# Half-product attention scores for all pairs of inner blocks, summed up in two PSUM banks

## The chip, the core and the metric

The kernel runs on one core of a Trainium2 chip. The metric is the device time of one execution in microseconds; lower is better. The median of three runs of the kernel before is 2275.2 us (2273.95 to 2275.97).

## What is computed

A stack of graph layers works on 3327 nodes with 256 features in float32, with one dense adjacency matrix. Layer 2, which the change touches, is masked dot-product attention followed by a residual and a layer norm:

```python
q = x @ Wq.T + bq
k = x @ Wk.T + bk
v = x @ Wv.T + bv
scores = q @ k.T / sqrt(256)
scores = where(adj > 0, scores, -9e15)
att = softmax(scores, axis=-1) @ v
x = layernorm(x + elu(att))
```

The other layers are a cosine attention (layer 0), a graph attention (layer 1) and three graph attentions in a row (layers 3a, 3b, 3c). They are the same in both kernels.

## The kernel before

The nodes are padded to 3328 and lie in 26 tiles of 128 (NT = 26) and in seven blocks of 512 (NB = 7, the last one 256 wide). A layer walks over its blocks `b` of query nodes, and within a block over the 26 tiles `j` of key nodes. One step (b, j) is one 128x512 tile of attention weights: key nodes on the partitions, query nodes along the columns. Since the weights come out transposed, they can be the left operand of the product with the values.

For layer 2 the query side is folded: `block2` makes `g` (gT in the profile), the 256 x 512 matrix that the keys' features `FT` are multiplied with. A score tile is thus a sum of two products of 128x128 weights with 512 columns, one for each half of the 256 features. `weights2` (lines 682 to 697) does that in one PSUM bank, lets ScalarE take the exponential out of the bank (L694), and VectorE multiplies by the mask (`masked`, L496).

Two neighbouring tiles j = 2p and 2p + 1 form a pair p. Seen as a pair, the scores are a 2x2 block product: two key tiles by two feature halves, times two feature halves by two query halves of 256 columns. Strassen's scheme in Winograd's form needs seven products of 128x128 by 256 columns for it, where the direct way needs eight (four of 512 columns). `pair_weights` (from L636) does it with seven. It needs sums of the query quarters, t1 to t4 (`sum_queries`, once per block, L583 to L586), and of the key quarters, s1 to s4 (`sum_keys`, L627 to L630, 128x128 each).

`by_pairs` (L607) says which pairs are made so. In the kernel before these are nine of the 13 pairs in the inner blocks 1 to 5 and four in block 0; the rest go through `weights2`. The nine are those for which a place was found to keep the key sums through the whole layer (`KPAIRS`: tags of weights that are no longer used, two "u" buffers, and unused columns of FT). `KSTEPS` says at which step of the layer each of them is summed.

`pair_weights` of before computes the products two to a bank, each into columns of its own: four banks, 7 products. ScalarE copies the first product out (L665). VectorE then adds the others one at a time to the running sums in SBUF (L666, L667, L668, L671, L672, L673, L676: seven adds of 256 columns, each with one operand in PSUM). Each of the two tiles then gets one exponential over 512 columns (L660) and one mask. It is a generator with three parts: the first four products when the step before the pair is made, the next two at the pair's first step, the last one at the second.

The attention product with the values is itself done in the seven-product way: `sums` (L883 to L886) makes four combinations of a pair's two weight tiles, and `products` (L935) issues 14 products of 128x128 by 128 or 129 columns for a pair, accumulated over the block in four PSUM banks of the pool `ps_o` (5 banks). The right operands come in part from DRAM (`fetch_tsum`, L857). All score work uses the pool `ps_b`: three banks, used in turn.

At step s the loop makes weights up to step s + 2 (`make_to`, LA = 2) before it issues the products of step s; they are issued at odd j for two tiles. A block that is done is normalised by `finish`, a generator that is advanced once per step of the next block: on ScalarE four scalings (L1181) and four exponentials for the ELU (L1247), on VectorE the joining of the seven products (L967 to L979), the ELU's adds (L1253, L1262), the statistics (L1109, L1110), the layer norm (L1291), and sums for the following layer.

Apart from the first few steps, a scheduler in the compiler orders each engine's instructions, so that instructions of several such parts lie between each other. The order on an engine is fixed when the program is built. Where two engines use the same PSUM bank the framework orders them by semaphores.

Of the kernel before, what the change touches and what calls it, by code (L numbers as in the profile page):

```python
# [8 lines left out]
F32 = mybir.dt.float32  # L9
# [4 lines left out]
AF = mybir.ActivationFunctionType  # L14
ALU = mybir.AluOpType
# [4 lines left out]
P = 128  # L20
D = 256
# [12 lines left out]
def gnn_stack(ctx: ExitStack, tc: tile.TileContext, a: dict, N: int, out: bass.AP):  # L34
# [8 lines left out]
    nc = tc.nc  # L43
    NT = (N + P - 1) // P
    NP = NT * P
    NB = (NP + CH - 1) // CH
# [11 lines left out]
    wts = ctx.enter_context(tc.tile_pool(name="wts", bufs=1))  # L58
    cols = ctx.enter_context(tc.tile_pool(name="cols", bufs=2))
    mpool = ctx.enter_context(tc.tile_pool(name="mpool", bufs=2))  # L60
    work = ctx.enter_context(tc.tile_pool(name="work", bufs=2))
# [4 lines left out]
    def bank(name):  # L66
        return ps_b.tile([P, CH], F32, tag="pb", name=name)
# [3 lines left out]
    start = tc.manual_schedule(  # L71
        engines={engines.PE, engines.Activation, engines.DVE, engines.Pool}
    )
# [419 lines left out]
    def masked(b, j, t_):  # L493
        wd = bw(b)
        e = work.tile([P, CH], F32, tag="e", name="e", bufs=9)
        nc.vector.scalar_tensor_tensor(  # L496
            e[:, :wd], t_[:, :wd], 0.0, mask(b, j), ALU.add, ALU.mult
        )
        return e
# [78 lines left out]
    def sum_queries(b):  # L578
# [13 lines left out]
    gsum, ksum = {}, {}  # L592
    KPAIRS = {
        1: "w_l0_wqk",
        2: "row_1",
        4: "scratch1",
        5: "scratch2",
        7: "u",
        8: "u",
        10: None,  # L600
        11: "w_l1_w",
# [3 lines left out]
    KSTEPS = {4: 5, 6: 7, 8: 8, 11: 10, 14: 1, 16: 2, 18: 4, NT + 14: 11, NT + 16: 12}  # L605

    def by_pairs(L, b, p):  # L607
        return L.key == "2" and b < NB - 1 and p in (KPAIRS if b > 0 else (5, 7, 8, 10))

    def keys_of(p):  # L610

# [4 lines left out]

    def sum_keys(p):
        a11, a12, a21, a22 = keys_of(p)
        if KPAIRS[p] is None:
            s1, s2, s3, s4 = wsum  # L620
        else:
            if KPAIRS[p] == "u":
                x = work.tile([P, 4, P], F32, tag="u", name="ksum", bufs=2)
            else:
                x = wts.tile([P, 4, P], F32, tag=KPAIRS[p], name="ksum")
            s1, s2, s3, s4 = (x[:, i, :] for i in range(4))
        nc.vector.tensor_tensor(s3, a11, a21, ALU.subtract)  # L627
        nc.vector.tensor_tensor(s1, a21, a22, ALU.add)
        nc.vector.tensor_tensor(s2, s1, a11, ALU.subtract)
        nc.vector.tensor_tensor(s4, a12, s2, ALU.subtract)  # L630
        ksum[p] = s1, s2, s3, s4

    def pair_weights(b, p):

        g, off = gq[b]
        b11, b12, b21, b22 = (g[:, h, i * D : (i + 1) * D] for h in range(2) for i in range(2))  # L636
        t1, t2, t3, t4 = gsum[b]
        a11, a12, a21, a22 = keys_of(p)
        s1, s2, s3, s4 = ksum[p]
        add = ALU.add  # L640
        x = [work.tile([P, CH], F32, tag="a", name="ex2", bufs=4) for _ in range(2)]
        c12, c22 = (t[:, D:] for t in x)

        def two(*pairs):
            ps = bank("ps2")
            for i, (l, r) in enumerate(pairs):
                nc.tensor.matmul(ps[:, i * D : (i + 1) * D], l, r, start=True, stop=True)
            return ps

        def add_two(out, x, ps):  # L650

            nc.vector.tensor_tensor(
                out.rearrange("p (i q) -> p i q", i=2),
                x.unsqueeze(1).to_broadcast([P, 2, D]),
                ps.rearrange("p (i q) -> p i q", i=2),
                add,
            )

        def weights(k):
            nc.scalar.activation(x[k], x[k], AF.Exp, bias=off, scale=1.0 / D**0.5)  # L660
            return masked(b, 2 * p + k, x[k])

        m12 = two((a11, b11), (a12, b21))
        m67 = two((s2, t2), (s3, t3))
        nc.scalar.copy(c22, m12[:, :D])  # L665
        nc.vector.tensor_tensor(x[0][:, :D], c22, m12[:, D:], add)  # L666
        nc.vector.tensor_tensor(c12, c22, m67[:, :D], add)  # L667
        nc.vector.tensor_tensor(c22, c12, m67[:, D:], add)  # L668
        yield
        m45 = two((a22, t4), (s1, t1))  # L670
        nc.vector.tensor_tensor(c12, c12, m45[:, D:], add)  # L671
        nc.vector.tensor_tensor(x[1][:, :D], c22, m45[:, :D], add)  # L672
        nc.vector.tensor_tensor(c22, c22, m45[:, D:], add)  # L673
        yield weights(1)
        m3 = two((s4, b22))
        nc.vector.tensor_tensor(c12, c12, m3[:, :D], add)  # L676
        yield weights(0)

    def weights2(b, j):

# [196 lines left out]
    def sums(b, e1, e2):  # L877

        hw = bw(b) // 2
        s3, s1, s2, s4 = (x[:, i, :hw] for x in two_slots("ssum") for i in range(2))  # L880
        e11, e21 = e1[:, :hw], e1[:, hw : 2 * hw]
        e12, e22 = e2[:, :hw], e2[:, hw : 2 * hw]
        nc.vector.tensor_tensor(s3, e11, e21, ALU.subtract)  # L883
        nc.vector.tensor_tensor(s1, e21, e22, ALU.add)
        nc.vector.tensor_tensor(s2, s1, e11, ALU.subtract)  # L885
        nc.vector.tensor_tensor(s4, e12, s2, ALU.subtract)  # L886
        return e11, e12, e22, s1, s2, s3, s4
# [19 lines left out]
    def products(pos, b, p, es, v):  # L907
        e11, e12, e22, s1, s2, s3, s4 = es
        t = tsums.pop((b, p))
        b1, b2 = v[2 * p], v[2 * p + 1]  # L910
        where = places(pos, b)


        todo = []
        x = {1: e11, 2: e12, 3: s4, 4: e22, 5: s1, 6: s2, 7: s3}
        y = {
            1: b1[:, H:],
            2: b2[:, H:],
            3: b2[:, :H],
            4: t[:, 3 * H + 1 :],  # L920
            5: t[:, : H + 1],
            6: t[:, H + 1 : 2 * H + 1],
            7: t[:, 2 * H + 1 : 3 * H + 1],
        }

        for k, i in (
            (1, 0), (1, 1), (2, 0), (7, 0), (7, 1), (6, 0), (6, 1),
            (2, 1), (5, 0), (5, 1), (4, 0), (4, 1), (3, 0), (3, 1),
        ):
            if i < len(where[k]):  # L930
                g, o = where[k][i]
                todo.append((g, o, x[k][:, i * P : (i + 1) * P], y[k]))
        banks = [t[0] for t in todo]
        for i, (g, o, x, y) in enumerate(todo):
            nc.tensor.matmul(  # L935
                o,
                x,
                y,
                start=(p == 0 and g not in banks[:i]),
                stop=(p == NT // 2 - 1 and g not in banks[i + 1 :]),  # L940
            )
# [539 lines left out]
    steps = [(L, b, j) for L in layers for b in range(NB) for j in range(NT)]  # L1481
    made = deque()

    pairs = {}

    def make(s):
        if s >= len(steps):
            return
        L, b, j = steps[s]
        make_weights(L, b, j)  # L1490
        if j % 2 and by_pairs(L, b, (j + 1) // 2):
            pairs[b, j + 1] = pair_weights(b, (j + 1) // 2)
            next(pairs[b, j + 1])

    cells = {}

# [3 lines left out]
    def make_weights(L, b, j):  # L1500
        if strassen(L, b) and j % 2 == 0 and kept.get((L.key, j // 2)) != b:
            fetch_tsum(L.key, b, j // 2)
        if by_pairs(L, b, j // 2):
            made.append(next(pairs[b, j - j % 2]))
            if j % 2:
                e1, e2 = made.pop(), made.pop()
                made.append(None)
                made.append(sums(b, e1, e2))
        else:
            if L.is_gat:  # L1510
                made.append(L.gat.weights(b, j))
                if deep(L) and strassen(L, b) and in_quad(b, j):
                    made[-1] = cells.setdefault((L.i, b, j // 2), []) if j % 2 else None
                    if j % 4 == 3:
                        v = quad(L.gat.quads, b, j).rearrange("p (a k) c -> p a k c", k=2)
                        for a_, x in enumerate(quad_sums(v)):
                            cells.pop((L.i, b, j // 2 - 1 + a_)).extend(x)
                    return
            else:
                made.append((weights0 if L.key == "0" else weights2)(b, j))  # L1520
            if strassen(L, b) and j % 2:
                e2, e1 = made.pop(), made.pop()
                made.append(None)
                made.append(sums(b, e1, e2))
# [36 lines left out]
    for s, (L, b, j) in enumerate(steps):  # L1561
# [5 lines left out]
        first = L.key == "0" and b == 0  # L1567
# [49 lines left out]
        if end:  # L1617

            k, h = divmod(2 * j, NT)
            for i in (h, h + 1):  # L1620
                for o in range(2 if k else 1):
# [5 lines left out]
                        start=(i == 0),  # L1627
# [70 lines left out]
        if L.key == "1" and (b, j) == (0, 22):  # L1698
            sum_weights(w[L.w])
        if L.key == "2" and b * NT + j in KSTEPS:  # L1700
            sum_keys(KSTEPS[b * NT + j])
        if L.key == "2" and (b, j) == (0, 3):
            sum_queries(0)
        if j == (25 if L.key == "1" else 22) and not end:
# [87 lines left out]
```

## Time and profile before

| | value |
|---|---|
| median of three runs | 2275.2 us |
| profiled execution: own time / span | 2274.9 us / 2273.1 us |
| PE busy | 2246.8 us, 99% |
| VectorE (DVE) busy | 1985.7 us, 87% |
| ScalarE (ACT) busy | 1236.6 us, 54% |
| granted TensorE clock | 0.998 |
| layer 2, about | 801 to 1368 us of the span |
| one inner block of layer 2 | 86 us |

PE is TensorE's matmuls, PEld its weight loads, DVE VectorE, ACT ScalarE, POOL GpSimd, SP the engine that issues DMAs. A group's row reads: line, engine, operation, tiles written <- read, shapes, count, busy time and mean duration, idle time of the engine just before and what ended it. A float32 product is two matmul instructions in the profile, each with its own weight load. Matmuls overlap each other's ends, so their cost in a stream is the distance from start to start and not the duration.

### The profile page before, as it was taken

How to read it: one execution, taken by the hardware profiler on the slowest of the kernel's cores; microseconds unless marked ns; L12 is line 12 of the kernel's file. 1: busy time of each engine (PE TensorE's matmuls, PEld its weight loads, DVE VectorE, ACT ScalarE, POOL GpSimd, SP SyncE). 2: the span in 40 equal slices, each digit the busy share in tenths (PEclk: the TensorE clock that was granted, in tenths of full speed). 3: DMA queues.
4: the chain of work that ended last, by engine and by line, in shares of the span. 5: the costliest groups of instructions: out<-in, count | busy, mean ns of one | idle time of the engine just before them, and what ended most of it. 6: DMA issues, size and time to landing. Idle time of an engine off the chain costs nothing. (4 is left out here: it accounts for less than half of the span.)

```text
span 2273.1 us, 41590 instructions
## 1 busy us (share of the span) xinstructions
PE 2246.8 (99%) x15183; PEld 1999.1 (88%) x15183; DVE 1985.7 (87%) x5407; ACT 1236.6 (54%) x2012; POOL 43.1 (2%) x196
## 2 busy tenths in 40 slices
PE   9999999999999999999999999999999999999997
PEld 7788888888888878888888899999999999999997
DVE  6889999966677767998988989999899999899997
ACT  4677777765455522232322335666666765666663
POOL 0000001000000000000000000000000000000000
PEclk9999999999999999999999999999999999999999
DMA  8655655522322232122122244445435545355542
GB/s 280 198 177 169 200 191 183 177 85 77 91 73 55 70 93 78 57 95 87 57 94 73 75 138 154 142 133 150 133 103 166 142 130 148 106 158 170 152 120 56
DMA packets 186208, 286.13 MB, mean 126 GB/s; under 512 B 80413, under 2 KB 105492, under 8 KB 181396
## 3 DMA queue, kind: packets, MB, share of 16 engines
q1 hardware_dynamic: 185732, 283.22, 41.3%
q8 instruction: 120, 1.97, 0.4%
q14 instruction: 84, 0.69, 0.1%
q10 hardware_dynamic: 272, 0.26, 0.0%
HBM read 228.21 MB, written 38.44 MB: 117 GB/s over the span
## 5 line engine op out<-in xcount | busy, mean ns | idle before, releaser
L787 ACT ACTIVATE re<-u,nrh,th 128x512 f32<-128x512 f32 (+1 forms) x728 | 532.7, 777 | 297.7 <-DVE e L800 146.8
L1657 PE MATMUL po<-v,e 128*128 128x257 f32 x1872 | 422.6, 381 | 1.0 <-ACT p L1181 0.8
L1657 PEld LDWEIGHTS po<-v,e 128*128 128x128 f32 x1872 | 352.6, 190 | 60.9 <-issue 9.8
L935 PE MATMUL po<-tsums,qsum 128*128 128x128 f32 (+1 forms) x2520 | 351.6, 275 | 3.1 <-DVE zs L970 1.2
L800 DVE SCALAR_TENSOR_TENSOR ft<-re,rh,mask 128x512 f32<-128x512 f32 x468 | 337.0, 741 | 3.0 <-ACT re L787 3.0
L935 PEld LDWEIGHTS po<-tsums,qsum 128*128 128x128 f32 x2520 | 315.4, 192 | 4.7 <-DVE qsum L873 1.5
L935 PE MATMUL po<-tsums,ssum 128*128 128x128 f32 (+1 forms) x2082 | 292.7, 276 | 2.7 <-DMA tsums<-t3a_d 1.0
L935 PE MATMUL po<-v,ft 128*128 128x129 f32 x1872 | 286.1, 276 | 0.8 <-DVE ft L800 0.3
L935 PEld LDWEIGHTS po<-tsums,ssum 128*128 128x128 f32 x2082 | 262.2, 192 | 5.7 <-DVE ssum L885 1.8
L935 PEld LDWEIGHTS po<-v,ft 128*128 128x128 f32 x1872 | 251.7, 192 | 5.7 <-DVE ft L800 1.1
L935 PEld LDWEIGHTS po<-v,e 128*128 128x128 f32 x1196 | 172.3, 191 | 37.6 <-issue 23.9
L935 PE MATMUL po<-v,e 128*128 128x129 f32 x1196 | 185.1, 275 | 0.0
L524 ACT ACTIVATE ex<-ps,rq 128x512 f32<-128x512 f32 (+1 forms) x183 | 118.9, 652 | 114.7 <-PE ps L511 111.8
L800 DVE SCALAR_TENSOR_TENSOR e<-re,rh,mask 128x512 f32<-128x512 f32 (+1 forms) x234 | 148.2, 655 | 35.1 <-PE po L1657 24.1
L511 PE MATMUL ps<-ft 128*128 128x512 f32 (+1 forms) x364 | 166.9, 564 | 0.0
L496 DVE SCALAR_TENSOR_TENSOR e<-ex,mask 128x512 f32<-128x512 f32 (+1 forms) x182 | 115.4, 648 | 49.0 <-ACT ex L694 31.8
L525 DVE SCALAR_TENSOR_TENSOR e<-ex,mask 128x512 f32<-128x512 f32 (+1 forms) x183 | 116.5, 642 | 31.0 <-ACT ex L524 30.4
L935 PE MATMUL po<-tsums,ft 128*128 128x128 f32 x936 | 143.5, 275 | 0.1
L686 PE MATMUL ps<-gT,ft 128*128 128x512 f32 (+1 forms) x336 | 129.8, 527 | 0.0
L935 PE MATMUL po<-v,qsum 128*128 128x128 f32 x840 | 128.3, 275 | 0.0
L935 PEld LDWEIGHTS po<-tsums,ft 128*128 128x128 f32 x936 | 123.5, 192 | 0.5 <-ACT p L1181 0.3
L660 ACT ACTIVATE ex<-ex,off 128x512 f32<-128x512 f32 x98 | 67.0, 716 | 101.7 <-DVE ex L676 69.1
(347 smaller groups left out, 3566.7 us busy)
## 6 DMA issues: line engine op xcount, KB each, us to landing
mask<-mask_d SPq DMA_DIRECT2D x30, 1664.0 KB
stage<-in_adj_a SPq DMA_DIRECT2D x78, 512.0 KB
tsums<-t_d SPq DMA_DIRECT2D x152, 256.5 KB
tsums<-t3a_d SPq DMA_DIRECT2D x77, 256.5 KB
tsums<-t3b_d SPq DMA_DIRECT2D x77, 256.5 KB
tsums<-t3c_d SPq DMA_DIRECT2D x77, 256.5 KB
mask_d<-mask SPq DMA_DIRECT2D x6, 1664.0 KB
u<-s_d SPq DMA_DIRECT2D x24, 256.0 KB
```

Source lines behind the costliest of these rows:

```text
L496: nc.vector.scalar_tensor_tensor(e[:, :wd], t_[:, :wd], 0.0, mask(b, j), ALU.add, ALU.mult)
L511: nc.tensor.matmul(ps[:, :wd], FT[j // 4][:, 0, (j % 4) * P : (j % 4 + 1) * P], FT[b][:, 1, :wd], start=True, stop=True,)
L524: nc.scalar.activation(t_[:, c], ps[:, c], AF.Exp, scale=rq[:, j : j + 1])
L525: nc.vector.scalar_tensor_tensor(e[:, c], t_[:, c], 0.0, mask(b, j)[:, c], ALU.add, ALU.mult)
L660: nc.scalar.activation(x[k], x[k], AF.Exp, bias=off, scale=1.0 / D**0.5)
L686: nc.tensor.matmul(ps[:, :wd], FT[j // 4][:, h, (j % 4) * P : (j % 4 + 1) * P], g[:, h, :wd], start=(h == 0), stop=(h == 1),)
L787: nc.scalar.activation(t_[:, :wd], self.u[b][:, :wd], AF.Relu, bias=self.nrh[:, j : j + 1], scale=self.th[:, j : j + 1],)
L800: nc.vector.scalar_tensor_tensor(e[:, :wd], t_[:, :wd], self.rh[:, j : j + 1], mask(b, j), ALU.add, ALU.mult,)
L935: nc.tensor.matmul(o, x, y, start=(p == 0 and g not in banks[:i]), stop=(p == NT // 2 - 1 and g not in banks[i + 1 :]),)
L1657: nc.tensor.matmul(pos[k], e[:, k * P : (k + 1) * P], V[L.i % 2][i], start=(i == 0), stop=(i == NT - 1),)
```

## The change

All pairs of the inner blocks 1 to 5 and the pairs 4 to 12 of block 0 are made from seven half-products. Key sums that aren't kept are computed for each use into a buffer of the tag "e". In `pair_weights` five of the seven products are accumulated one after the other in one half of one bank (`r`): each running sum is copied out by ScalarE before the next product is added to it. The second product takes the other half of that bank. The last two (s1·t1 and s4·b22) are summed up in a second bank (`q`). VectorE adds three times instead of seven. One exponential half is read straight out of the bank.

The parts are issued at other places too: the first at the odd step before the pair (ahead of the end of the pair before), the second and third in the middle of `products` of an earlier pair (before its fifth and tenth product), the last when the pair's second tile is made.

```diff
     def by_pairs(L, b, p):
-        return L.key == "2" and b < NB - 1 and p in (KPAIRS if b > 0 else (5, 7, 8, 10))
+        return L.key == "2" and b < NB - 1 and p < NT // 2 and (b > 0 or p > 3)
...
     def sum_keys(p):
         a11, a12, a21, a22 = keys_of(p)
-        if KPAIRS[p] is None:
+        kept_in = KPAIRS.get(p, "e") if p not in ksum else "e"
+        if kept_in is None:
             s1, s2, s3, s4 = wsum
...
+            elif kept_in == "e":
+                x = work.tile([P, 4, P], F32, tag="e", name="ksum", bufs=9)
...
-        ksum[p] = s1, s2, s3, s4
+        return s1, s2, s3, s4
+
+    inner = deque()
...
-        s1, s2, s3, s4 = ksum[p]
...
+        s1, s2, s3, s4 = ksum[p] if p in ksum else sum_keys(p)
...
-        m12 = two((a11, b11), (a12, b21))
-        m67 = two((s2, t2), (s3, t3))
-        nc.scalar.copy(c22, m12[:, :D])
-        nc.vector.tensor_tensor(x[0][:, :D], c22, m12[:, D:], add)
-        nc.vector.tensor_tensor(c12, c22, m67[:, :D], add)
-        nc.vector.tensor_tensor(c22, c12, m67[:, D:], add)
-        yield
-        m45 = two((a22, t4), (s1, t1))
-        nc.vector.tensor_tensor(c12, c12, m45[:, D:], add)
-        nc.vector.tensor_tensor(x[1][:, :D], c22, m45[:, :D], add)
-        nc.vector.tensor_tensor(c22, c22, m45[:, D:], add)
-        yield weights(1)
-        m3 = two((s4, b22))
-        nc.vector.tensor_tensor(c12, c12, m3[:, :D], add)
-        yield weights(0)
+        def put(out, l, r, first=False):
+            nc.tensor.matmul(out, l, r, start=first, stop=True, skip_group_check=True)
+
+        ps = bank("ps2")
+        r, m2 = ps[:, :D], ps[:, D:]
+        put(r, a11, b11, first=True)
+        put(m2, a12, b21)
+        nc.scalar.copy(c11, r)
+        nc.vector.tensor_tensor(c11, c11, m2, ALU.add)
+        yield
+        put(r, s2, t2)
+        nc.scalar.copy(c12, r)
+        yield
+        put(r, s3, t3)
+        q = bank("ps3")[:, :D]
+        put(q, s1, t1, first=True)
+        nc.scalar.copy(c22, r)
+        nc.vector.tensor_tensor(c22, c22, q, ALU.add)
+        yield
+        put(r, a22, t4)
+        put(q, s4, b22)
+        nc.scalar.activation(c21, r, AF.Exp, bias=off, scale=scale)
+        nc.scalar.activation(c22, c22, AF.Exp, bias=off, scale=scale)
+        e2 = masked(b, 2 * p + 1, x[1])
+        nc.vector.tensor_tensor(c12, c12, q, ALU.add)
+        nc.scalar.activation(x[0], x[0], AF.Exp, bias=off, scale=scale)
+        yield masked(b, 2 * p, x[0]), e2
...
         for i, (g, o, x, y) in enumerate(todo):
+            if i in (4, 9) and inner:
+                next(inner[0])
             nc.tensor.matmul(
...
+        if j % 2 and s + 1 < len(steps):
+            ln, bn, jn = steps[s + 1]
+            if by_pairs(ln, bn, jn // 2):
+                pairs[bn, jn] = pair_weights(bn, jn // 2)
+                next(pairs[bn, jn])
+                inner.append(pairs[bn, jn])
         make_weights(L, b, j)
-        if j % 2 and by_pairs(L, b, (j + 1) // 2):
-            pairs[b, j + 1] = pair_weights(b, (j + 1) // 2)
-            next(pairs[b, j + 1])
```

In the text below, c11, c12, c21 and c22 are the four quarters of a pair's two score tiles; "the c12 copy" is ScalarE's copy into that quarter, ADD11, ADD22 and ADD12 are VectorE's three adds into c11, c22 and c12, and s2·t2 is the product of s2 and t2.

More of the change, by code (lines that the diff above doesn't have):

```diff
@@ L618, in sum_keys @@
         a11, a12, a21, a22 = keys_of(p)
-        if KPAIRS[p] is None:
+        kept_in = KPAIRS.get(p, "e") if p not in ksum else "e"
+        if kept_in is None:
             s1, s2, s3, s4 = wsum
         else:
-            if KPAIRS[p] == "u":
+            if kept_in == "u":
                 x = work.tile([P, 4, P], F32, tag="u", name="ksum", bufs=2)
+            elif kept_in == "e":
+                x = work.tile([P, 4, P], F32, tag="e", name="ksum", bufs=9)
             else:
-                x = wts.tile([P, 4, P], F32, tag=KPAIRS[p], name="ksum")
+                x = wts.tile([P, 4, P], F32, tag=kept_in, name="ksum")
             s1, s2, s3, s4 = (x[:, i, :] for i in range(4))
@@ L638, in pair_weights @@
         a11, a12, a21, a22 = keys_of(p)
-        s1, s2, s3, s4 = ksum[p]
-        add = ALU.add
+        s1, s2, s3, s4 = ksum[p] if p in ksum else sum_keys(p)
+        scale = 1.0 / D**0.5
         x = [work.tile([P, CH], F32, tag="a", name="ex2", bufs=4) for _ in range(2)]
[L642 to L661, printed above, removed]
-        m12 = two((a11, b11), (a12, b21))
-        m67 = two((s2, t2), (s3, t3))
@@ L676, in pair_weights @@
-        nc.vector.tensor_tensor(c12, c12, m3[:, :D], add)
-        yield weights(0)
+        c11, c12, c21, c22 = (t[:, h * D : (h + 1) * D] for t in x for h in range(2))
+        def put(out, l, r, first=False):
[6 more added lines that the diff above has]
+        nc.vector.tensor_tensor(c11, c11, m2, ALU.add)
@@ L1503, in make_weights @@
         if by_pairs(L, b, j // 2):
-            made.append(next(pairs[b, j - j % 2]))
-            if j % 2:
-                e1, e2 = made.pop(), made.pop()
+            if j % 2 == 0:
                 made.append(None)
-                made.append(sums(b, e1, e2))
+            else:
+                g = pairs.pop((b, j - 1))
+                inner.remove(g)
+                made.append(sums(b, *next(g)))
         else:
@@ L1700, in gnn_stack @@
         if L.key == "2" and b * NT + j in KSTEPS:
-            sum_keys(KSTEPS[b * NT + j])
+            p = KSTEPS[b * NT + j]
+            ksum[p] = sum_keys(p)
         if L.key == "2" and (b, j) == (0, 3):
```

## The prediction

> **What bounds the kernel now.** I read the page's engine shares first, then the busy time by stage, then the timeline of one stretch of layer 2, then the groups of that layer by form.
>
> ```profile
> PE 2246.8 (99%) x15183; PEld 1999.1 (88%) x15183; DVE 1985.7 (87%) x5407; ACT 1236.6 (54%) x2012; POOL 43.1 (2%) x196
> ```
>
> TensorE is busy 99% of the span, so a nanosecond of matmul removed is a nanosecond saved, unless TensorE starts to wait. Next, four stretches of layer 2 (window, its length, then busy us of PE, PEld, DVE, ACT, POOL, clock, DMA):
>
> ```profile
> 837.00:920.00 83.00, 83.00 (x494) 67.04 (x493) 65.18 (x192) 24.87 (x45) 0.51 (x3) 1.00 0.24 72
> 920.00:1003.00 83.00, 82.76 (x523) 70.45 (x522) 73.05 (x225) 23.76 (x45) 0.20 (x2) 1.00 0.25 82
> 1003.00:1086.00 83.00, 82.81 (x521) 70.76 (x520) 73.03 (x226) 23.30 (x44) 0.20 (x2) 1.00 0.24 79
> 1169.00:1252.00 83.00, 82.99 (x515) 69.91 (x514) 73.61 (x229) 23.13 (x43) 0.20 (x2) 1.00 0.24 75
> ```
>
> PE has at most 0.24 us of 83 to give; DVE stands at 88%, ACT at 29%, DMA at a quarter. Layer 2 is bound by TensorE, with DVE close behind. The price of a matmul comes from start to start in the timeline (start, duration, last column xcount):
>
> ```profile
> 1000.86 3.60 PE L686 MATMUL ps<-gT,ft 128*128 128x512 f32 x8
> 1004.29 1.03 PE L647 MATMUL ps<-gT,ft 128*128 128x256 f32 x4
> 1005.16 1.03 PE L647 MATMUL ps<-gsums,ksum 128*128 128x256 f32 x4
> 1006.02 0.83 PE L935 MATMUL po<-v,e 128*128 128x129 f32 x6
> ```
>
> Eight 512-column instructions take 3.43 us, 0.429 each; eight 256-column ones 1.73, 0.216 each. Each fp32 product is two instructions (x8 is two tiles of two products). An attention product (L935) is two at 0.111, from 1006.69 to 1007.58 for eight.
>
> What the other engines pay, by form, in layer 2 (count | busy us, mean ns | idle before):
>
> ```profile
> L665 ACT COPY ex<-ps 128x256 f32<-128x256 f32 x49 | 18.1, 370 | 119.3 <-PE ps L647 90.2 <-DVE rs_y L153 28.9 <-DVE var L1281 0.2
> L660 ACT ACTIVATE ex<-ex,off 128x512 f32<-128x512 f32 x98 | 67.0, 716 | 101.7 <-DVE ex L676 69.1 <-DVE ex L673 32.6
> L694 ACT ACTIVATE ex<-ps,off 128x256 f32<-128x256 f32 x26 | 12.3, 471 | 21.6 <-PE ps L686 19.3 <-DVE k_3b L210 2.0 <-DVE ssum L884 0.4
> L667 DVE TENSOR_TENSOR ex<-ex,ps 128x256 f32<-128x256 f32 x49 | 20.3, 414 | 5.0 <-PE ps L647 4.7
> L844 DVE TENSOR_TENSOR tsum<-v 128x128 f32<-128x128 f32 x14 | 4.0, 285 | 0.9 <-DMA t_d<-tsum 0.8
> ```
>
> And what a wait costs, at one of the few that TensorE has here:
>
> ```profile
> 942.78 0.41 DVE L666 TENSOR_TENSOR ex<-ex,ps 128x256 f32<-128x256 f32 x1
> 943.24 0.30 PEld L647 LDWEIGHTS ps<-gT,ksum 128*128 128x128 f32 x2 [0.65 <-DVE ex L666]
> 943.25 0.70 PE L647 MATMUL ps<-gT,ksum 128*128 128x256 f32 x2 [0.24 <-DVE ex L666]
> ```
>
> L666 ends at 943.19; the weight load starts 0.05 us later, no longer under a matmul: its 0.1 us come on top. Such bank waits cost about 0.3 to 0.5 us per block, 1.8 in all.
>
> **What the Trainium skill says.** "TensorE: Matmul & The Clock Gate", Back-to-back issue gap, gives N/2.4 + 2.5 ns when warm: 215.8 for 512 columns, 109 for 256. The trace has twice that, each product split in two instructions besides; the ratio of the sizes, on which I rest, agrees. "PSUM — Partial Sum Buffer", PSUM bank collisions, wants two engines kept apart by bank, whichever columns they touch. So in the changed kernel the third product, into the left half of the bank, has to wait also for the DVE read of its right half. In the built program's order it does wait for DVE; the trace before has no such pair. "VectorE: DVE Perf Modes", Rules for kernel authors, says of chained DVE operations to minimize their count; here 256-column adds follow each other every 0.33 us (1008.17, 1008.50, 1008.83), so fewer adds do free DVE.
>
> **The change part by part.** The built program says how much moves: 74 pairs instead of 49.
>
> 1. TensorE, on the path. 25 pairs (4 more in each of five inner blocks, 5 more in block 0) lose four 512-column products and get seven 256-column ones: 8 x 0.429 - 14 x 0.216 = 0.41 us, times 25 = **-10.2 us**. The 49 old pairs keep their seven.
>
> 2. DVE, beside it. PSUM adds fall from 343 to 222, at 0.33: -40 us. Key sums for pairs without kept ones are made anew: 25 x 4 subtractions at 0.2 (start to start, 941.91 to 942.11) to 0.285 (duration): +20 to +28. Net -12 to -20 of some 480 us; this makes no time itself, as TensorE covers it, but shortens the DVE queue.
>
> 3. ACT, beside it. Copies 49 to 222, +173 x 0.37 = 64 us; exponentials lose 74 of 512 (-53) and gain 148 of 256 at 0.47 (+70). Net +81 over 530 us: from 29% to some 45%, hidden while TensorE doesn't wait for it.
>
> 4. The new waits. Each pair has three round trips: product into the bank, ACT copy, next product into the same columns. One takes from the end of issue 0.16 (0.379 duration less 0.216) + 0.04 (matmul end to ACT: 1002.74 to 1002.78 at an L694) + 0.37 + 0.05 = **0.63 us**. What stands between them in the built order is 2.2 us typically before the third product, and 2.4 before the fifth (ending in the exponential). Between s2·t2 and s3·t3 it is five attention products (1.12 us) in most pairs, four (0.88) in some, three (0.66) in 19. The first two cover it; the 19 leave the weight load bare: 19 x 0.1 = **+1.9 us** at most. Waiting there holds the whole TensorE queue, and the attention products with it.
>
> 5. The queues behind. ACT's c12 copy stands after the earlier pair's half exponential and in two or three pairs per block after its full one (0.72); there DVE's add stands ahead of the mask, so ACT is free before the product ends. DVE per pair: 7 operations of 0.33 and two masks of 0.60 (1004.90 to 1005.50), 3.5 us, against 6.1 of TensorE. While a finished block is normalised it gets up to 7.8 in one pair (finish, key sums); the lag reaches some 1.7 us, and the first add, for which the third product waits, comes 0.1 to 0.2 us late in two pairs per block: 5 x 0.3 = **+1.5 us**. Both ends: nothing, if the order hides it; 1.5 us per block, 9 in all, if ACT's elu exponentials (each waits for a DVE release, up to 2.3 us now by the waits of L1247) stand ahead of a copy at the wrong time.
>
> 6. What goes: the bank waits above, **-1.8 us**, since only two banks per pair are turned over, not four. Unless ADD22 is late instead: it has 1.5 to 2.8 us of cover after s1·t1.
>
> 7. Costed at nothing: the first half of a pair moves ahead of the earlier pair's end (same products, other place); some tsums fetches go one or two places later in SP's queue, behind stores (DMA is at a quarter and a fetch is due a pair later; if that cover goes, up to a few tenths a block); key sums take a tenth use of nine "e" buffers, whose oldest reader is a pair back. POOL is unchanged. After layer 2 all engines have the same order.
>
> Sum: -10.2 + 1.9 + 1.5 - 1.8 = **-8.6 us**, on the profiled execution: span 2273.1, its own time 2274.9, to 2266.3. The median of the runs, 2275.2, is 0.3 above it: **2266.5**.
>
> **The rivals.** (a) *The round trips eat most of the gain.* For: c12's copy has the least slack of all, 0 to 0.5 us, and ACT must be idle at that moment. Against: ACT at 45%, in an order that puts the copy early. At 0.05 to 0.13 us a pair, 4 to 9 us go: 2270.7 to 2275. (b) *Slower: the round trip of s2·t2 becomes the bound.* One mechanism: in the pairs during a block's normalisation (some nine of 13) the copy stands in ACT behind an instruction that itself waits for DVE. Price: 0.3 us in each of about 50 pairs is 15 us, less 10.2: 2280. It decides from 0.14 us per pair (10.2/74). Against: DVE has less to do than now. (c) *More than the sum:* no new wait, old ones gone: 2263. (d) That the pairs aren't made so is excluded by the built order.
>
> **How the numbers follow.** A measurement of this kernel tells about 0.2%, 4.6 us, from no change. Forecast and near it (2262 to 2270.6): 0.71; (a): 0.18, of which nearly all lies up to 2275 and counts as no change; (b): 0.08; (c) below 2262: 0.03. Faster 0.74, same 0.17, slower 0.09. The range 2262 to 2275 leaves out (b), (c) and the upper rest of (a).
>
> **What would show it.** Right: matmuls 128x512 of layer 2 down to the eight tiles of block 0 besides block setup; an inner block every 84.4 us instead of 86 (from copy to copy of L961, 901.8, 987.9, 1074.0); PE still at 99%; DVE in an inner block near 84%, ACT near 45%. Waits of the pair's products on ACT's copies near 2 us in total, on DVE's adds as much. Wrong: waits on the c12 copy of tenths of a us in most pairs, blocks at 86 us or more, or PE idle in the windows above 1 us per block.

## The result, and the profile after

The kernel became slower: 2279.2 us (median of 22 runs, 2276.9 to 2280.8) against 2275.5 for the kernel before in the same measurement (22 runs, 2273.3 to 2277.8). The ratio is 1.0015, 95% interval 1.0009 to 1.0022. The forecast was 2266.5 with a range of 2262 to 2275. Repeated beside later experiments, the ratio was 1.0018 (1.0011 to 1.0025).

First the engine shares on the page of the changed kernel, then four stretches of its layer 2 (window, length, busy us of PE, PEld, DVE, ACT, POOL, clock, DMA share, GB/s):

```profile
PE 2246.5 (99%) x15333; PEld 2029.3 (89%) x15333; DVE 1967.1 (86%) x5386; ACT 1317.7 (58%) x2259; POOL 42.8 (2%) x196
```

```profile
838.00:921.00 83.00, 82.74 (x538) 74.84 (x538) 70.14 (x224) 37.94 (x88) 0.51 (x3) 1.00 0.25 72
922.00:1005.00 83.00, 82.02 (x532) 73.68 (x531) 67.86 (x210) 37.15 (x85) 0.20 (x2) 1.00 0.27 80
1009.00:1092.00 83.00, 82.45 (x534) 74.05 (x533) 68.29 (x211) 37.51 (x87) 0.20 (x2) 1.00 0.27 82
1175.00:1258.00 83.00, 82.35 (x534) 74.13 (x533) 67.91 (x212) 37.66 (x86) 0.20 (x2) 1.00 0.24 71
```

DVE and ACT do about what was forecast: DVE fell from 73 to 68 us of 83 (82%, forecast near 84%), ACT rose to 37.5, which is 45%. But PE, which had at most 0.24 us of idle time in 83, now has 0.55 to 0.98 in the inner blocks. And those are only the waits that show as idle.

"Busy" hides part of them, since matmuls overlap. So I took layer 2 apart by start-to-start distances: the sum, over all matmuls, of the usual distance of their shape (0.216 us at 256 columns, 0.429 at 512, 0.112 at 128) is the **work**; what the actual distances have above it is the **stall**. A block is counted from the first matmul of `block2` (L541) to the same one of the next block, as a mean over the five periods that begin with blocks 1 to 5. The first of these periods is longer than the others (89.0 us before, 89.8 after); the other four are 85.9 before and 86.7 after. Distances a little under the usual one are not set against the stall, so work and stall add up to some 0.1 us more than the period.

| per inner block | before | after |
|---|---|---|
| period, us | 86.5 | 87.3 |
| work | 85.97 | 84.33 |
| stall | 0.67 | 3.11 |
| of it waits ahead of a product's first instruction | 0.26 | 1.82 |
| of it late second instructions (bare weight load) | 0.40 | 1.29 |

The work fell by 1.64 us, four pairs at 0.41. The stall rose by 2.44. Over the five blocks the periods make +3.8 us, and the spans differ by +3.6: the rest nearly cancels (the changed kernel begins layer 2 1.0 us later, is 0.7 us quicker in block 0 and 0.5 us quicker from block 6 on).

The groups of layer 2 by form (count | busy us, mean ns | idle time before, and what ended it):

```profile
L660 ACT COPY ex<-ps 128x256 f32<-128x256 f32 x74 | 27.4, 370 | 82.3 <-PE ps L650 80.7
L673 DVE TENSOR_TENSOR ex<-ex,ps 128x256 f32<-128x256 f32 x74 | 30.6, 414 | 2.8 <-PE ps L650 2.8
L666 DVE TENSOR_TENSOR ex<-ex,ps 128x256 f32<-128x256 f32 x74 | 30.6, 414 | 9.1 <-PE ps L650 4.5 <-ACT ex L665 4.2 <-issue 0.2
L842 DVE TENSOR_TENSOR tsum<-v 128x128 f32<-128x128 f32 x14 | 4.0, 287 | 7.2 <-DMA t3a_d<-tsum 6.4 <-DMA t_d<-tsum 0.8
L684 PE MATMUL ps<-gT,ft 128*128 128x512 f32 x32 | 14.7, 592 | 0.0
```

The first three rows (c12's copy, ADD12, ADD22) have their forecast counts and prices. L684 shows that only eight tiles of 512 columns are still made the direct way (32 instructions, four each). The row to stop at is L842, the first subtraction of a value-sum for the next layer (`combine`, L844 in the kernel before). There its 14 instructions waited 0.9 us in all; now 7.2, of which 6.4 are for a store to DRAM. DVE stands still in five places, once per inner block, for 1.1 to 1.5 us.

This is one of them, in the order of time (start, duration, engine, line):

```profile
1023.72 0.32 SPq L851 DMA_DIRECT2D t3a_d<-tsum  x1
...
1027.46 0.29 DVE L842 TENSOR_TENSOR tsum<-v 128x128 f32<-128x128 f32 x1 [1.09 <-DMA t3a_d<-tsum]
...
1028.87 0.41 DVE L673 TENSOR_TENSOR ex<-ex,ps 128x256 f32<-128x256 f32 x1
...
1029.32 0.72 ACT L674 ACTIVATE ex<-ex,off 128x512 f32<-128x512 f32 x1 [1.74 <-DVE ex L673]
1029.34 0.73 PEld L650 LDWEIGHTS ps<-gT,ft 128*128 128x128 f32 x4 [0.30 <-DVE ex L673]
...
1029.95 0.35 ACT L665 COPY ex<-ps 128x256 f32<-128x256 f32 x1
1030.08 0.69 DVE L496 SCALAR_TENSOR_TENSOR e<-ex,mask 128x512 f32<-128x512 f32 x1 [0.79 <-ACT ex L674]
1030.35 0.30 PEld L650 LDWEIGHTS ps<-gsums,ft 128*128 128x128 f32 x2 [0.28 <-ACT ex L665]
...
1030.68 0.41 DVE L666 TENSOR_TENSOR ex<-ex,ps 128x256 f32<-128x256 f32 x1
...
1031.15 0.30 PEld L650 LDWEIGHTS ps<-gT,ksum 128*128 128x128 f32 x2 [0.50 <-DVE ex L666]
```

A finished block makes two value-sums. Both use the same buffer of the tag "x4k" (two buffers, the other is held by gT). The second may only be written when the store of the first has landed; here it starts 3.74 us after that store's issue. DVE waits 1.09 us for it, and ADD12 (L673), which stands behind it in the queue, comes late. PE waits 0.30 us for ADD12. So does ScalarE's exponential L674; behind that one stand c22's copy (L665) on ScalarE and, through the mask that reads it (L496), ADD22 (L666) on VectorE. PE waits for these too, 0.28 and 0.50 us.

The kernel before has the same buffer and the same store, but hardly a wait (0.10 us in the block shown, none in the other four). The two orders on DVE, with SP's rows where they matter, tell why. Before:

```profile
1021.15 0.28 DVE L844 TENSOR_TENSOR tsum<-v 128x128 f32<-128x128 f32 x1
...
1022.70 0.28 DVE L852 TENSOR_TENSOR tsum<-tsum,v 128x128 f32<-128x128 f32 x1
...
1023.05 0.32 SPq L853 DMA_DIRECT2D t3a_d<-tsum  x1
...
1026.74 0.29 DVE L844 TENSOR_TENSOR tsum<-v 128x128 f32<-128x128 f32 x1
```

After:

```profile
1020.82 0.28 DVE L842 TENSOR_TENSOR tsum<-v 128x128 f32<-128x128 f32 x1
...
1022.36 0.41 DVE L666 TENSOR_TENSOR ex<-ex,ps 128x256 f32<-128x256 f32 x1
...
1022.59 0.32 SPq L855 DMA_DIRECT2D tsums<-t_d  x1
1022.70 0.42 DVE L881 TENSOR_TENSOR ssum<-e 128x256 f32<-128x256 f32 x1
1023.03 0.42 DVE L882 TENSOR_TENSOR ssum<-e 128x256 f32<-128x256 f32 x1
1023.37 0.28 DVE L850 TENSOR_TENSOR tsum<-tsum,v 128x128 f32<-128x128 f32 x1
```

Before, the last subtraction (L852) comes 1.55 us after the first, and from its start it takes DVE 3.9 us until it is ready for the second value-sum. After, an add and two weight sums have slipped in front of the last subtraction (L850): 2.55 us (the same in all five blocks), and 3.0 us are left from there (1027.46 - 1.09 - 1023.37). From the first subtraction to the second value-sum DVE's work is the same, 5.4 to 5.5 us before and 5.55 after. So it is not that DVE has less to do in this stretch: a microsecond of its work has moved from behind the store to ahead of it.

Counted from the store's issue, DVE was ready for the second value-sum after 3.5 to 3.6 us in the kernel before, and is ready after 2.65 us in the changed one. By the landing events in the traces, these stores land 3.0 to 3.6 us after their issue in the kernel before, and 3.6 to 4.1 us in the changed one. The cover had been only just enough; 0.9 us of it went, and the store became some 0.5 us slower besides. In the changed kernel SP issues a fetch (L855) 1.1 us ahead of each of these five stores, in the kernel before none within 3 us of them. That may be the reason; no run tests it.

A second place is that of the key sums made anew (rows of VectorE and of the product that waits):

```profile
1000.40 0.42 DVE L1109 BATCH_NORM_STATS2 bn<-y 128x6 f32<-128x256 f32 x1
1000.74 0.27 DVE L630 TENSOR_TENSOR ksum<-ft 128x128 f32<-128x128 f32 x1
1000.93 0.17 DVE L1110 BATCH_NORM_AGGREGATE st<-bn 128x2 f32<-128x6 f32 x1
1001.03 0.25 DVE L631 TENSOR_TENSOR ksum<-ft 128x128 f32<-128x128 f32 x1
...
1001.43 0.67 PE L650 MATMUL ps<-gsums,ksum 128*128 128x256 f32 x2 [0.19 <-DVE ksum L631]
1001.53 0.28 DVE L632 TENSOR_TENSOR ksum<-ksum,ft 128x128 f32<-128x128 f32 x1
```

They are issued with their pair, so they stand in the queue behind the normalisation of the finished block, immediately ahead of the products that read them. PE waits for them in two of the four such pairs of each inner block.

In all, the stall of an inner block after the change goes to: key sums (L631, L632) 0.79 us, ADD11 (L657) 0.63, ADD12 0.57, ADD22 0.36, c12's copy 0.23, and the rest 0.5, most of it other copies by ScalarE (gT 0.22, c22's 0.15). Second instructions left bare are counted with what was waited for ahead of them.

### The profile page after: what moved, and what is told of

Read it like the earlier page. It is cut to its first block, busy times and chain, and to the rows that moved or that the text cites. A ratio compares the mean times of both kernels' runs of the same rounds, so it can differ in the third digit from the quotient of the medians.

```text
span 2276.7 us, 42083 instructions
## 1 busy us (share of the span) xinstructions
PE 2246.5 (99%) x15333; PEld 2029.3 (89%) x15333; DVE 1967.1 (86%) x5386; ACT 1317.7 (58%) x2259; POOL 42.8 (2%) x196
## 5 line engine op out<-in xcount | busy, mean ns | idle before, releaser
L935 PE MATMUL po<-tsums,ssum 128*128 128x128 f32 (+1 forms) x2082 | 310.4, 275 | 2.4 <-DVE ssum L883 1.2
L935 PEld LDWEIGHTS po<-tsums,ssum 128*128 128x128 f32 x2082 | 280.5, 192 | 10.6 <-DVE ssum L883 2.0
L496 DVE SCALAR_TENSOR_TENSOR e<-ex,mask 128x512 f32<-128x512 f32 (+1 forms) x182 | 117.7, 647 | 31.5 <-ACT ex L674 16.2
L467 DVE CUSTOM_DVE_ANT_0 acc<-acc,stage 128x1024 uint16<-128x1024 uint16 (+1 forms) x168 | 108.5, 646 | 12.6 <-DMA stage<-in_adj_a 9.4
L650 PE MATMUL ps<-gsums,ksum 128*128 128x256 f32 x408 | 115.1, 389 | 1.8 <-DVE ksum L631 0.9
```

The costliest lines, as they stand in the source:

```text
L467: nc.vector.tensor_tensor(acc, acc, st[:, h * wd : (h + 1) * wd], ALU.add)
L496: nc.vector.scalar_tensor_tensor(e[:, :wd], t_[:, :wd], 0.0, mask(b, j), ALU.add, ALU.mult)
L650: nc.tensor.matmul(out, l, r, start=first, stop=True, skip_group_check=True)
L935: nc.tensor.matmul(o, x, y, start=(p == 0 and g not in banks[:i]), stop=(p == NT // 2 - 1 and g not in banks[i + 1 :]),)
```

## The experiments

The theory to be tested (A in the expectations): the extra stall is made in VectorE's queue. Rivals: (B) the new form is free, the 25 new pairs cost more than they save through their key sums, (C) it is the round trips over ScalarE. The experiments ran in three series (e1 to e4; e5 to e7 with the changed kernel again; e8, e9 and e6 again). The kernel before had 2274.1, 2275.6 and 2274.5 us in them, so each ratio is to the kernel before of its own series. All from medians; blocks and stall are read from one profiled execution of each run as above. The two pairs of runs of one kernel (after and after again, e6 and e6 again) agree in them to 0.1 us. Where an expectation speaks of e6's blocks of 85.2 us, it counts the last four periods alone.

| run | us | ratio, 95% interval | block | stall |
|---|---|---|---|---|
| e1, new form, old pairs | 2274.3 | 1.0002 (0.9994 to 1.0010) | 86.7 | 0.7 |
| e2, old form, all pairs | 2327.3 | 1.0233 (1.0219 to 1.0247) | 94.5 | 10.4 |
| e3, own slot for the second value-sum | 2270.8 | 0.9987 (0.9980 to 0.9993) | 86.0 | 1.8 |
| e4, borrowed key sums | 2271.8 | 0.9989 (0.9982 to 0.9995) | 86.3 | 2.2 |
| e5, e3 and e4 together | 2271.1 | 0.9981 (0.9973 to 0.9989) | 85.6 | 1.5 |
| e6, e3 and key sums a pair earlier | 2271.8 | 0.9983 (0.9977 to 0.9990) | 85.8 | 1.6 |
| e6 again | 2271.1 | 0.9985 (0.9977 to 0.9993) | 85.8 | 1.6 |
| e7, e6 and two products later | 2271.7 | 0.9985 (0.9979 to 0.9992) | 86.0 | 1.8 |
| e8, e6 and another bank | 2275.8 | 1.0005 (0.9996 to 1.0013) | 86.8 | 2.7 |
| e9, before with the own slot | 2274.6 | 1.0000 (0.9992 to 1.0008) | 86.5 | 0.6 |
| after again | 2279.4 | 1.0018 (1.0011 to 1.0025) | 87.2 | 3.1 |

**e1: the form alone.**

```diff
-        return L.key == "2" and b < NB - 1 and p < NT // 2 and (b > 0 or p > 3)
+        return L.key == "2" and b < NB - 1 and p in (KPAIRS if b > 0 else (5, 7, 8, 10))
```

> The new form of pair_weights (running sums in two banks, copies by ScalarE) for the same 49 pairs as before. Theory A (TensorE waits for things that stand in VectorE's queue: an add behind a wait for a store, late key sums, the first add): TensorE's work is that of before, no key sums are made anew, but the waits of the form stay, some 1 to 1.5 us per inner block: 2280 to 2284. Rival B (the form is free, the 25 new pairs with their key sums cost the time): 2275 as before. Rival C (the copy round trips on ScalarE cost most): 2280 to 2284 too, but with the waits in the trace ended by ScalarE.

Measured: 2274.3, no difference from the kernel before, as rival B said. Two stretches of its layer 2:

```profile
920.00:1003.00 83.00, 82.82 (x521) 70.48 (x521) 63.00 (x187) 33.84 (x72) 0.20 (x2) 1.00 0.26 82
1003.00:1086.00 83.00, 82.83 (x521) 70.50 (x520) 62.75 (x188) 34.23 (x73) 0.20 (x2) 1.00 0.25 79
```

DVE drops to 63 us and ACT rises to 34, and TensorE stalls about as much as before (0.74 us a block; 0.67 before), though for other things: 0.44 of it is on c12's copy, while the kernel before had 0.37 on an add (L666 there) that is gone. So three round trips per pair cost about what the old bank waits did, where nothing else delays them. Theory C falls, and my theory A as worded for this run too: the form brings no extra delay by itself. Nor does less work for DVE: of these kernels this one gives it least, but in its order it comes to the second value-sum 5.1 us after the store's issue and doesn't wait. The first half of B holds; whether the key sums make all the rest, e3 to e6 tell.

**e2: the count alone**, the form of before with all 74 pairs.

> The old form (four banks, seven adds by VectorE) for all 74 pairs. It has the 10.2 us less of TensorE's work, but 25 x 7 more adds of 0.33 and 25 x 4 key subtractions of 0.2 on VectorE: in an inner block 75.8 + 4 x 3.1 = 88 us of VectorE's work. Theory A and the sum of VectorE's work: VectorE becomes the bound, blocks of 88 us or more, 2285 to 2292. Rival C (the new form is to blame, more pairs by themselves pay): 2266 to 2270.

Measured: 2327.3, far beyond what any theory expected. Two stretches, and the largest waits of TensorE between 864 and 1300 us (waiting engine, tile and line <- releaser: total us, times, longest):

```profile
900.00:983.00 83.00, 77.49 (x472) 68.59 (x471) 76.09 (x244) 23.32 (x45) 0.10 (x1) 0.96 0.25 78
983.00:1066.00 83.00, 77.57 (x494) 68.41 (x493) 77.53 (x249) 23.53 (x45) 0.20 (x2) 1.00 0.23 76
```

```profile
PEld po L938 <- DVE e L496: 24.9, 26, 1.8
PE po L938 <- DVE e L496: 22.7, 20, 1.7
```

DVE is busy 92 to 93% and has become the bound: the attention products wait for the mask (L496), which ends the chain of a pair's adds. Not all of the loss is that: between the spans, 41 us have come by the last score product of layer 2; 11 come after it, and their cause was not looked into. And in three places of layer 2 this run's granted clock falls to a half for 3.4 us each (the 0.96 above is one stretch with two of them), as in no other run's layer 2: about 5 us at most, an estimate from these figures. Still, the two halves of the change are not independent: seven adds for every pair cost 53 us, the form alone nothing, both together 3.6. The form makes the count possible; what it doesn't do is make VectorE's order good.

**e3: another slot for the second value-sum**, so that it need not wait for the store of the first.

```diff
+        elif key == "3a" and p % 2:
+            t = work.tile([P, 4 * H + 1], F32, tag="stage", name="tsum", bufs=4)
```

> The kernel after, with the second of the two value sums that each finished block of layer 2 stores for layer 3a in a buffer of the tag stage instead of x4k, so that it doesn't have to wait for the first one's store. Theory A: the 1.1 us for which VectorE stood at it goes, with the waits of the pair behind it (ADD12, ADD22, c22 copy, ADD11, some 1.2 us with their bare weight loads) in each of five blocks: 2279 less 5 to 6.5, 2272.5 to 2274. Rival C (form and ScalarE): 2278 to 2279, since other work takes its place.

Measured: 2270.8, ratio 0.9987. The same place in its timeline:

```profile
1021.89 3.84 SPq L853 DMA_DIRECT2D t3a_d<-tsum  x2
...
1024.12 0.29 DVE L844 TENSOR_TENSOR tsum<-v 128x128 f32<-128x128 f32 x1
...
1025.86 0.41 DVE L673 TENSOR_TENSOR ex<-ex,ps 128x256 f32<-128x256 f32 x1
...
1027.34 1.03 PE L650 MATMUL ps<-gT,ft 128*128 128x256 f32 x4
1027.99 0.41 PEld L650 LDWEIGHTS ps<-gsums,ft 128*128 128x128 f32 x2
1028.20 0.59 PE L650 MATMUL ps<-gsums,ft 128*128 128x256 f32 x2
1028.42 0.41 PEld L650 LDWEIGHTS ps<-gT,ksum 128*128 128x128 f32 x2
1028.63 0.59 PE L650 MATMUL ps<-gT,ksum 128*128 128x256 f32 x2
```

The first row holds the issues of both stores. The second value-sum starts 2.2 us after the first store's issue, long before that has landed, and nobody waits: ADD12 is done 1.07 us before the product behind it, and the eight 256-column instructions that had met three waits run in one stream. In the trace the waits on ADD12, c22's copy and ADD22 are gone altogether (1.1 us a block), the key sums' stay. One wait of DVE on a DMA was worth 1.3 us a block, 6.5 in all by the blocks (6.4 by the ratios; 5 to 6.5 were expected). e9 below shows that this was the change's own loss.

**e4: no key sums made anew.** The unkept pairs borrow those of pair 5, so their scores are not the reference's; only the time counts here.

```diff
-        s1, s2, s3, s4 = ksum[p] if p in ksum else sum_keys(p)
+        s1, s2, s3, s4 = ksum[p if p in ksum else 5]
```

> The kernel after, with the key sums of pair 5 used for all pairs that have no kept sums: the 100 key subtractions made in place are left out, everything else stays. Theory A: the waits for key sums go, 0.8 us per inner block, some of the first adds behind them too: 2279 less 4 to 6, 2273 to 2275. Rival C: no change, 2278 to 2279.

Measured: 2271.8, ratio 0.9989. The stall falls by 0.9 us a block. DVE still waits for the store, but for 3.1 us in five blocks instead of 6.4, because the last subtraction is back at 1.54 us after the first, and DVE is ready 3.3 us after the store's issue. ADD12 and ADD22 are no longer late, ADD11 is (1.5 us a block). So the key sums cost in two ways, by their own lateness and by pushing others.

**e5: both cures.**

```diff
+        elif key == "3a" and p % 2:
+            t = work.tile([P, 4 * H + 1], F32, tag="stage", name="tsum", bufs=4)
...
+        s1, s2, s3, s4 = ksum[p if p in ksum else 5]
```

> The changed kernel with both suspected causes taken away at once: the second value-sum of a finished block gets its own slot (as in e3_tsum_other_slot) and the pairs without kept key sums borrow those of pair 5 (as in e4_borrowed_key_sums; this leaves out 100 key subtractions, so these pairs' scores are not the reference's). Theory A (two separate delays in VectorE's queue, one on the store's release, one on key sums made late): the savings of the two add up: 3.5 to 5 us from the first, 3 to 5 us from the second, so 8 us under the changed kernel of the same chip, about 2267; inner-block stall of TensorE near 1.0 us (3.1 after), work 84. Rival R (one shared shortage of VectorE, either cure gives the same slack): no more than the better of the two alone, 2270 to 2271, stall 1.8.

Measured: 2271.1, 8.3 us under the changed kernel of the same series, as the theory's sum said. That was luck, since its terms were wrong. By the blocks, e3 alone had given 6.5 us, not 3.5 to 5, and e4 alone 4.9; together they give 8.5, not 11.4. The two causes overlap: without key sums made anew the wait for the store is already halved (e4), and both delay the same adds in one queue. A stall of 1.5 us remains that neither explains; 0.8 of it is ADD11.

**e6: key sums a pair earlier**, with the own slot; nothing is left out.

```diff
+        if j % 2 == 0 and s + 2 < len(steps):
+            ln, bn, jn = steps[s + 2]
+            if by_pairs(ln, bn, jn // 2) and jn // 2 not in ksum:
+                early_sums[bn, jn // 2] = sum_keys(jn // 2)
...
+        s1, s2, s3, s4 = ksum[p] if p in ksum else early_sums.pop((b, p))
```

> The changed kernel with the own slot for the second value-sum, and with the key sums of pairs without kept ones issued one pair earlier, so that they are done before the pair's products need them; nothing is left out. Theory A (it is the place of the key sums in VectorE's queue, not their amount, that costs): TensorE no longer waits for key sums, near the run with borrowed sums, 2266 to 2269, stall 1.0 to 1.3 us per inner block. Rival R (it is the amount of VectorE's work): no better than with the own slot alone, 2270 to 2272, and the waits move to the adds.

Measured: 2271.8, and 2271.1 in the third series. No wait on a key sum is left, and the blocks are 0.2 us shorter than with the slot alone; but the waits on ADD11 doubled, from 0.5 to 1.0 us a block, as the rival said of the amount of work, and the stall of 1.6 us is above the theory's 1.0 to 1.3. By the medians the step from e3 to e6 can't be told from nothing.

> The kernel of e6_sums_a_pair_earlier once more, beside these two on their chip: 0.998 to 0.999 of the kernel before, inner blocks of 85.2 us.

e6 is 0.17% and 0.15% faster than the kernel before, 0.33% faster than the changed one of its series (2279.4), and leaves nothing out. It is the version to keep of those tried; e3, with two lines, is nearly as good.

**e7: the inner products later**, before the seventh and twelfth attention product.

```diff
-            if i in (4, 9) and inner:
+            if i in (6, 11) and inner:
```

> As e6_sums_a_pair_earlier, and the pair's two later groups of score products are issued two attention products later (6 and 11 in place of 4 and 9), so that the first add into the bank has more time before the third product needs it, and the last group less before the exponentials. Theory A (what is left are the bank waits on the first add, 0.5 us per block with the bare weight loads): stall falls by 0.3 to 0.5 us per block, 1.5 to 2.5 us less than e6, about 2265. Rival R (the cover is only moved: the fifth product now waits on the copy of the corner sum instead): same as e6 within 1 us or up to 3 us slower, with waits on that copy.

Measured: 2271.7, the same. ADD11 0.99 instead of 1.02 us a block, c12's copy 0.42 instead of 0.29: the rival's reading, the cover is only moved.

**e8: the second product into the other bank.**

```diff
-        r, m2 = ps[:, :D], ps[:, D:]
+        qs = bank("ps3")
+        r, m2, q = ps[:, :D], qs[:, D:], qs[:, :D]
...
-        q = bank("ps3")[:, :D]
```

> As e6_sums_a_pair_earlier, and the second product of a pair goes into the free right half of the pair's second PSUM bank (taken three products earlier for it) instead of beside the running sum: the third product then waits only for ScalarE's copy, and the first write after VectorE's first add is s1·t1, a product later. Theory A (the rest of the stall, 1.0 us per inner block, is the shared bank: the third product waits for an add whose columns it doesn't touch): stall falls from 1.6 to 0.6 to 0.9 us per block, 3 to 5 us less than e6 on the same chip, about 2267. Rival R (the add is late in itself and s1·t1 waits as long, or the bank held longer makes a later tile wait): stall 1.4 or more, within 1 us of e6.

Measured: 2275.8, 4.6 us more than e6 beside it: neither expectation has that, though the rival named the kind of wait. The waits on ADD11 are gone, as meant. But the pool has three banks, and a pair now takes its second one when it begins; that is the bank of the pair before, which ScalarE's exponential of c21 (L671) reads last:

```profile
984.11 0.60 PE L651 MATMUL ps<-gT,ft 128*128 128x256 f32 x2
...
985.17 0.47 ACT L671 ACTIVATE ex<-ps,off 128x256 f32<-128x256 f32 x1
...
985.70 0.30 PEld L651 LDWEIGHTS ps<-gT,ft 128*128 128x128 f32 x2
985.70 0.70 PE L651 MATMUL ps<-gT,ft 128*128 128x256 f32 x2
```

The weight load starts 0.06 us after the exponential's end (985.64), and no wait is printed; but the two instructions last 0.70 instead of 0.60, the weight load of the second being bare. There are some nine such products a block; together they stall for 1.6 us, more than ADD11 had cost. The Trainium skill, "PSUM — Partial Sum Buffer", PSUM bank collisions, guards a bank and not its columns. The traces agree in what the programs wait for: in the changed kernel the third product waits for ADD11, which reads the other half of its bank (0.63 us a block), and here the second product, in a right half, waits for a reader of the left one. This run adds that parting two readers by another bank took a bank that was not to spare.

**e9: the own slot in the kernel before.**

> The kernel before with the own slot for the second value-sum. Theory A (the wait for the store came with the change, since VectorE reaches that place earlier; before it, VectorE waited there for 0.8 us in all): no gain, 0.9990 to 1.0005 of the kernel before, inner blocks of 86 us with a stall of 0.6 to 0.7 us. Rival R (the slot helps any version, so that what e3 gained is not the change's doing): 0.997 to 0.9985, 4 to 6 us less, as there.

Measured: 2274.6 against 2274.5, ratio 1.0000. The slot helps only where DVE waits for the store. (The reason in the expectation is not what the orders show: counted from the first subtraction, DVE is back no sooner in the changed kernel; the store leaves later and lands later, as shown above.)

**The changed kernel again**, as the mark for e5 to e7.

> The changed kernel itself on the chip of these three, as their common mark: 1.0015 of the kernel before (2277 to 2280). If it lies within 0.05% of the kernel before instead, then the savings are counted from that.

Measured: 2279.4, its blocks and stalls as in the first profile.

## Why the prediction was wrong

- Step 1 was right: 1.64 us of matmul work a block, 0.41 a pair, over 20 inner pairs 8.2 us.
- Step 2's amounts were right (DVE 18.6 us less, forecast 12 to 20); its conclusion, that a shorter sum is a shorter queue, failed. The order on DVE changed with the sum, and order is what its readers wait for.
- Step 3 was right in its sum: ACT +81 us. It hides all but 0.45 us a block, the waits on ScalarE's copies into c12 and gT; e1, with no slower time, shows that the copies are cheap where VectorE is not late.
- Step 4 was half right. The bare weight loads after c12's copy came (17 in five blocks, 1.2 us, forecast at most 1.9 for all). Those after the gT copies and the key sums, and after adds that are late for another reason than step 5's, were not counted: late second instructions rose from 24 to 76 over the five blocks, +4.4 us.
- **Step 5, the queue behind, is the one that failed.** It took DVE's lag to be a matter of the sum of its work, and put it at 1.5 us in all (the first add late) and its upper end, 9 us, down to ScalarE's ELU. ADD11 alone cost 0.63 us a block, 3.2 in five. And DVE came to wait itself, 1.3 us a block for a store, with ADD12 and ADD22 late behind it. The waits ahead of a first instruction rose from 0.26 to 1.82 us a block, 7.8 us in five: 7.8 + 4.4 = 12.2 against a gain of 8.2. Of the stall of 3.1 us a block, 2.35 is on VectorE's adds and key sums. The ELU can have a part only in the waits on copies, which are small.
- Step 6 failed by the condition that it named itself: ADD22 is late, and costs 0.36 us a block, about what the old bank waits had cost.
- **Step 7 failed too: it costed the key sums at nothing** apart from their DVE time, and looked at their buffers. They are operands of the next product: 0.79 us a block. And a buffer that the diff doesn't touch, the value-sums' slot, was in no list at all. The row of it was in the prediction (L844, 0.9 us idle, "<-DMA t_d"); I read it as a price and not as a wait that another order could make long: 6.5 us in all, by e3.
- Rival (b) had nearly the number, 2280, with the wrong mechanism: c12's copy costs 0.23 us a block. Its mechanism, a copy in ACT's queue behind an instruction that waits for DVE, is seen at another copy, c22's, once per block and for 0.15 us. That its number was near is luck. The signs given as proof of error, blocks of 86 us or more, came true: 86.7 from copy to copy.

Not settled: why the scheduler put an add and two weight sums ahead of the last subtraction (that e4 returns it to its old place shows only that the key sums are part of it), and why the stores land later. And 0.9 us a block above the kernel before remain in e6; e7 and e8 moved them and did not remove them.

## What to carry to other kernels

An edit that gives an engine less to do can also reorder its queue, as here. Where that engine's results are needed just in time by another, list every wait that its queue could meet on any resource, DMA releases of shared buffers first, with its present margin (here a store that landed after 3.0 to 3.6 us against 3.5 to 3.6 of other work), and not only those in the lines changed. An operand made just in time belongs on the path of its reader, whatever its engine's load. And of two cures in one queue, measure both together: here their gains overlapped.

## What the runs showed of the hardware that I had not expected

A TensorE that is "busy" all the time can be stalling. Two stretches, of e6 again and of e8, which have the same products in a block:

```profile
1003.00:1086.00 83.00, 82.98 (x546) 75.24 (x545) 69.50 (x221) 38.32 (x87) 0.20 (x2) 1.00 0.26 81
```

```profile
1003.00:1086.00 83.00, 83.00 (x536) 74.54 (x536) 69.67 (x217) 38.74 (x87) 0.20 (x2) 1.00 0.26 82
```

PE's busy time says 83.00 of 83 for the kernel whose blocks are 1 us longer: a wait that is just met leaves the second weight load bare, 0.10 us each time, and the matmul's modelled duration covers it. The count of matmuls (546 against 536) and PEld's busy time tell the two apart. The Trainium skill, "Perfetto Trace Analysis", Identifying the Most-Contended Engine, says to judge TensorE by the busy share of its weight loads, and by its operations as a share of the peak, and not by matmul time. As to the weight loads, the traces of three kernels with the same products agree: PEld is busy 74.0 us of 83 in the changed kernel's inner blocks (mean of the last three windows shown), 74.5 in e8, 75.2 in e6, in the order of their blocks of 87.3, 86.8 and 85.8 us.
